# A four-layer network on one core: the first layer's weight fold is moved ahead of the norm and onto ScalarE, and GpSimd builds the convolution matrices

## The chip, the cores and the metric

The kernel runs on one core of a Trainium2 chip. The metric is the device time of one execution in microseconds (us). The five engines of a core have an instruction queue each: TensorE (in profiles PE for matmuls, PEld for its weight loads), VectorE (DVE), ScalarE (ACT), GpSimd (POOL) and SyncE (SP), which here only issues transfers. Each engine takes its own instructions strictly in the order in which they stand in its queue; an instruction that waits for another engine holds up all that stand behind it on its own. Matmul results are in PSUM, which GpSimd doesn't reach in this kernel; VectorE or ScalarE copy them to SBUF.

## What is computed

Sixteen images of 256 channels by 32 x 32 positions go through four layers, all in float32:

```
# layer 0: group norm (8 groups), then self-attention over the 1024 positions
xn = group_norm(x, gamma, beta)
q, k, v = split(einsum('bchw,oc->bohw', xn, w_qkv) + b_qkv)
x = x + w_proj @ (softmax(q^T k / sqrt(C)) v) + b_proj
# layer 1: a gate from the channels' mean and maximum, through two 3x3 convolutions
weight3 = relu(conv3x3(concat([mean, max]), w1, b1))
x = x * sigmoid(conv3x3(mean + max + weight3, w2, b2))
# layer 2: group norm and self-attention again, with weights of its own
# layer 3: attention with 32-wide q and k, logits clipped to [-10, 10], times gamma[0], plus x
```

## The kernel before

**Weights are folded first.** For layers 0 and 2 the kernel works with products of the weights: with M = Wq^T Wk / sqrt(C) the logits are x^T M x, and with Wv and Wproj multiplied beforehand the projection after the attention is gone. `fold(nm, which, base)` makes these once, at the start. `transposed(j)` turns the j-th 256 x 256 weight block (0 is q, 1 is k, 2 is v) on TensorE, four 128 x 128 transposes (L311), and copies the result from PSUM with two VectorE copies (L316). `multiplied` makes a product with eight matmuls as the profile counts them (L322) and scales it out of PSUM with two VectorE instructions (L329). Between them stand `right_sums` (L288 to L291: four sums of weight blocks, on VectorE for M, on GpSimd for the value product), a small bias product `tbp` (L344, scaled at L351) and another, `brp` (L365, added at L372). `fold` is a generator: it yields between its steps.

**Layer 0's norm.** `head(b)` fetches sample b, starts the load of a second copy of it in another layout (`load_tokens`, `xr`), and runs `group_norm`: `bn_stats` over four quarters of the sample on VectorE (L114), a chain of small VectorE instructions that spreads the group's numbers over the partitions (L117 to L134), the power -1/2 on GpSimd (`rstd`, L138), three more small VectorE instructions (L141 to L144), and then the sample itself: channels 0 to 127 on VectorE (L145) and channels 128 to 255 on ScalarE (L146), one instruction of 128 x 1024 each.

**Order.** The order in which instructions are traced is the order that a scheduler starts from; it may bring instructions forward inside an engine's queue, except where `tc.keep_in_program_order` or a dependency added by hand forbids it. `in_turn` runs several generators a step each in rotation. At the very start it runs `head(0)` and `fold("l0", ...)`, so VectorE's queue has the statistics of sample 0 and the copies of the fold interleaved. After that, two streams of samples (even and odd, `stream(0)` and `stream(1)`) run in rotation, together with `later()`, which holds what isn't needed at once: `head(1)` and `fold("l2", ...)`, then `fold3()` (layer 3's weights and biases: `w3qk` copies on GpSimd L410, `bias3` L417 and L426, `qb`, `bcol3` and `strips` L434 to L437 and L380), then `build_toep`, then `checks()`.

**What follows the fold for sample 0.** `attend` makes four sums of sample blocks (`combine`, L909 to L912, tiles `xs` and `x`), then `seven`: each 2 x 2 block product is made with seven products in place of eight (all through L562, tiles `tb`, `ta`, `tc`, `tf` for x^T M, `vb`, `va`, `vc`, `vf` for the values, `sb`, `sa`, `sc`, `sf` for the logits); ScalarE copies some out of PSUM and VectorE adds the others (L612). Then come exponentials (L691, L693) and the weighted values (`weighted`: `b`, `af`, `c`, with sums of exponentials `cb` and others on VectorE, L707, L708, L753, L758).

**The convolution matrices.** The 3 x 3 convolutions of layer 1 are matmuls with 128 x 32 matrices `toep`. `Const.build_toep` builds three of them from the nine taps each: one VectorE instruction per tap (L95: where the index equals the tap, the weight, else 0), one addition for all but the first tap (L98), and three copies of the last matrix (L101). `gate_of` reads them (L169, L182). `n_ok` counts sums in range (L787, L823, L876, on GpSimd); it is read at the end.

**Queues of transfers.** SP issues nearly all; ScalarE's queue has one half of layer 0's weights and half of sample 0 at the start. The sequence on SP is weights of layer 0, sample 0, small constants, sample 1, weights of layers 2 and 3, index tables, and the second copies of samples 0 to 2.

Of the kernel before, what the change touches and what calls it, by code (L numbers as in the profile page):

```python
# [12 lines left out]
AF = mybir.ActivationFunctionType  # L13
ALU = mybir.AluOpType
# [3 lines left out]
C = 256  # L18
CC = C // P
# [37 lines left out]
class Const:  # L57
# [26 lines left out]
    def build_toep(self, tc, work, tidx):  # L84

        nc = tc.nc
        for k in range(3):
            for tap in range(9):
                w = self.sc[:, S_W1 + 9 * k + tap : S_W1 + 9 * k + tap + 1]
                if tap == 0:  # L90
                    one = self.toep[:, k, :]
                else:
                    one = work.tile([P, STRIP], FP, tag="tap", name=f"tap_{k}_{tap}")
                tc.keep_in_program_order(
                    nc.vector.tensor_scalar(one, tidx, float(tap), w, ALU.is_equal, ALU.mult)  # L95
                )
                if tap:
                    nc.vector.tensor_tensor(self.toep[:, k, :], self.toep[:, k, :], one, ALU.add)  # L98
            yield
        for g in range(1, NG):  # L100
            nc.vector.tensor_copy(self.toep[:, 2 + g], self.toep[:, 2])  # L101
        nc.vector.tensor_scalar(self.neg_b2, self.sc[:, S_B2 : S_B2 + 1], -1.0, None, ALU.mult)
        yield


def group_norm(nc, k, small, xt, out, gamma, beta, nm, keep=None):

# [2 lines left out]
    for c in range(CC):  # L112
# [29 lines left out]
    bb = small.tile([P, CC], FP, tag="bb", name=f"bb_{nm}")  # L142
    nc.vector.tensor_tensor(bb, gm, a, ALU.mult)
    nc.vector.tensor_tensor(bb, k.vec[:, :, beta], bb, ALU.subtract)  # L144
    nc.vector.tensor_scalar(out[:, 0], xt[:, 0], a[:, 0:1], bb[:, 0:1], ALU.mult, ALU.add)  # L145
    nc.scalar.activation(  # L146
        out[:, 1], xt[:, 1], AF.Identity, bias=bb[:, 1:2], scale=a[:, 1:2]
    )
    yield


# [50 lines left out]
def fast_path(nc, tc, k, bad, x, w_l0, w_l2, w_l3, qk_bias, v_bias, tap_idx, out):  # L202
# [7 lines left out]
    with ExitStack() as ctx:  # L210
# [83 lines left out]
        def whole(w, nm):  # L294
# [3 lines left out]
            nc.vector.tensor_tensor(full[:, 0, P:], w[:, 1, P:], w[:, 0, P:], ALU.subtract)  # L298
            return full

        def fold(nm, which, base):


# [3 lines left out]
            def transposed(j):  # L307
                for o in range(CC):
                    ps = bank(f"wtp_{nm}_{j}_{o}")
                    for c in range(CC):  # L310
                        nc.tensor.transpose(  # L311
                            ps[:, c * P : (c + 1) * P],
                            w[:, c, j * C + o * P : j * C + (o + 1) * P],
                            k.ident,
                        )
                    nc.vector.tensor_copy(wt[:, j, o, :], ps[:, :C])  # L316

            def multiplied(dst, left, right, scale):
                for c in range(CC):
                    ps = bank(f"fold_{nm}_{c}")  # L320
                    for o in range(CC):
                        nc.tensor.matmul(  # L322
                            ps[:, :C],
                            left[:, o, c * P : (c + 1) * P],
                            right[:, o, :],
                            start=(o == 0),
                            stop=(o == CC - 1),
                        )
                    nc.vector.tensor_scalar(dst[:, c, :], ps[:, :C], scale, None, ALU.mult)  # L329

            transposed(0)
            yield
# [9 lines left out]
            for c in range(CC):  # L342
                for o in range(CC):
# [4 lines left out]
                        start=(o == 0),  # L348
                        stop=(o == CC - 1),
                    )  # L350
            nc.vector.tensor_scalar(tb, ps[:, :CC], C**-0.5, None, ALU.mult)  # L351
            yield
            transposed(2)
            yield
# [582 lines left out]
        def attend(xt, y, weights, lane, nm, then):  # L937
# [39 lines left out]
                then(h, tt.rearrange("p h c n -> p h (c n)"))  # L977
            count(ri, nm)

        def head(b):  # L980

            fetch(b)
# [2 lines left out]
            xr = tokens[b] = load_tokens(b)  # L985
            keep = tc.keep_in_program_order if b == 1 else None
            yield from group_norm(
                nc, k, small, by_chunk, by_chunk, L0_GAMMA, L0_GAMMA + 1, f"l0_{b}", keep
            )
            ready[b] = xt, xr  # L990

# [468 lines left out]
            if first in running:  # L1460
                running.remove(first)

        for _ in in_turn([head(0), fold("l0", 0, L0_GAMMA)]):
            pass


# [328 lines left out]
```

## Time and profile before

| | us |
|---|---|
| median of three runs | 2697.19 |
| lowest and highest of them | 2692.31, 2699.09 |
| the profiled execution | 2694.99 |
| its span in the profile | 2693.2 |
| mean granted TensorE clock in it | 0.997 of full speed |

The span is what the profile covers; the time of an execution has a little around it. The profile's parts that matter here are the busy time of each engine as a share of the span; a table of stages, in which each row is a stretch of time with the busy time and number of instructions of each engine, the granted clock of TensorE and the transfers; the chain of work that ended last, followed back from the end; and the timeline, in which each row has start, duration, engine, line, operation, output<-input, shape and count, and in brackets how long the engine had been idle before and what ended that. Buffer numbers are left out of names, so layer 0's and layer 2's weights are both `raw_l`, and two samples' tiles have one name.

Two more rows of groups help to read what follows (busy time and mean ns of one, after the bar):

```profile
L138 POOL TENSOR_TENSOR rstd_l<-ve_l,neg_half 128x2 f32<-128x2 f32 x32 | 22.2, 695 | 1388.4 <-DVE ve_l L134 1388.4
...
L410 POOL COPY w3qk<-w 128x64 f32<-128x64 f32 x4 | 0.8, 237 | 0.0
```

They are GpSimd's: its work is small, 45.3 us of the span, and its instructions have durations that depend little on their size.

### The profile page before, as it was taken

The page shows a single profiled execution, that of the slowest core. Times are in us where ns is not written, and L with a number is a line of the kernel's source. Part 1 is how long each engine was busy: PE and PEld are TensorE (multiplying, and loading weights), DVE is VectorE, ACT ScalarE, POOL GpSimd, SP SyncE. Part 2 cuts the span into 40 slices and gives each one's busy share as a digit, 9 for nine tenths or more (in the row PEclk, how much of TensorE's full clock was granted, in tenths as well). Part 3 has the DMA queues.
Part 4 walks back from the last instruction along what each step waited for, and adds up shares of the span by engine and source line. Part 5 has one row for each costly group of instructions (what it writes and reads, how often), then busy time and mean ns, then how long its engine had stood idle before and what let it go on. Part 6 is the DMA issues. An engine that isn't in the chain of part 4 may idle for free.

```text
span 2693.2 us, 47725 instructions
## 1 busy us (share of the span) xinstructions
PE 2654.9 (99%) x18998; PEld 2364.0 (88%) x18998; DVE 2152.2 (80%) x4244; ACT 1328.5 (49%) x2813; POOL 45.3 (2%) x118
## 2 busy tenths in 40 slices
PE   7999999999999999999999999999999999999998
PEld 6888988888988889889899898998989889898897
DVE  7988886888778887788867888678886788878777
ACT  3454455544455445544455545455454544545443
POOL 1000000000000000000000000000000000000000
PEclk9999999999999999999999999999999999999999
DMA  4021111212011120211201212112111121101111
GB/s 115 1 63 48 56 32 27 61 48 64 24 47 48 42 77 9 55 48 48 63 15 50 63 33 64 31 33 64 48 48 32 32 64 48 48 17 32 48 40 41
DMA packets 135878, 123.07 MB, mean 46 GB/s; under 512 B 12768, under 2 KB 126688, under 8 KB 135648
## 3 DMA queue, kind: packets, MB, share of 16 engines
q1 hardware_dynamic: 133776, 118.76, 15.9%
q8 instruction: 152, 2.49, 0.4%
q10 hardware_dynamic: 1872, 1.18, 0.1%
q14 instruction: 78, 0.64, 0.1%
HBM read 69.58 MB, written 50.33 MB: 45 GB/s over the span
## 4 chain that ended last, share of the span: by engine, by line
PE 80%; DVE 14%; ACT 3%; issue 2%; DMA 0%; POOL 0%; DVEq 0%; SPq 0%; ACTq 0%
PE b_l L562 15%; PE af_l L562 11%; PE c_l L562 11%; PE sb_l L562 10%; PE sc_l L562 8%; PE sf_l L562 4%; PE sa_l L562 3%; PE vb_l L562 3%; PE tb_l L562 2%; PE s L1099 2%; PE vc_l L562 2%; PE tc_l L562 2%; DVE e_l L612 1%; DVE vt L612 1%; PE qk L1073 1%
## 5 line engine op out<-in xcount | busy, mean ns | idle before, releaser
L681 ACT COPY e_l<-sb_l 128x512 f32<-128x512 f32 x384 | 222.3, 584 | 218.1 <-PE sb_l L562 216.9
L562 PE MATMUL sb_l<-t_l,x 128*128 128x256 f32 x1024 | 262.0, 386 | 0.3
L562 PE MATMUL b_l<-vt,e_l 128*128 128x128 f32 x2048 | 251.8, 275 | 0.0
L562 PEld LDWEIGHTS b_l<-vt,e_l 128*128 128x128 f32 x2048 | 244.2, 192 | 5.4 <-issue 2.3
L562 PEld LDWEIGHTS sb_l<-t_l,x 128*128 128x128 f32 x1024 | 180.5, 191 | 40.1 <-ACT e_l L681 11.2
L691 ACT ACTIVATE e_l<-e_l 128x512 f32<-128x512 f32 x256 | 160.7, 629 | 86.4 <-DVE e_l L612 85.5
L693 ACT ACTIVATE e_l<-e_l 128x1024 f32<-128x1024 f32 x128 | 135.4, 1058 | 118.3 <-DVE e_l L612 118.3
L562 PE MATMUL c_l<-tv,cb_l 128*128 128x129 f32 x1504 | 185.1, 275 | 0.2 <-DVE cb_l L707 0.2
L562 PEld LDWEIGHTS c_l<-tv,cb_l 128*128 128x128 f32 x1504 | 176.6, 191 | 6.9 <-PE qk L1073 3.1
L612 DVE TENSOR_TENSOR e_l<-sc_l,e_l 128x512 f32<-128x512 f32 x128 | 87.7, 685 | 115.3 <-PE sc_l L562 113.6
L478 ACT ACTIVATE xr<-xr,bstrip 128x128 f32<-128x128 f32 (+1 forms) x376 | 134.0, 440 | 43.5 <-DVE xr L485 43.5
L932 ACT COPY vt<-vb_l 128x512 f32<-128x512 f32 x141 | 82.7, 587 | 142.8 <-PE vb_l L562 141.7
L1115 ACT ACTIVATE e<-s 128x512 f32<-128x512 f32 x256 | 132.0, 605 | 28.6 <-PE s L1099 27.9
L562 PE MATMUL af_l<-tv,e_l 128*128 128x128 f32 x1024 | 131.6, 278 | 4.3 <-ACT e_l L691 4.3
L562 PE MATMUL sc_l<-tc_l,xs_l 128*128 128x256 f32 x512 | 133.1, 382 | 2.3 <-DVE vt L612 2.3
L763 ACT COPY acc_l<-c_l 128x256 f32<-128x256 f32 x94 | 34.6, 368 | 201.5 <-DVE ri_l L762 151.7
L562 PE MATMUL sc_l<-t_l,xs_l 128*128 128x256 f32 x512 | 133.0, 382 | 0.8
L562 PE MATMUL sa_l<-t_l,x 128*128 128x256 f32 x512 | 132.1, 380 | 0.0
L1124 DVE TENSOR_SCALAR e<-e 128x1024 f32<-128x1024 f32 x128 | 82.9, 683 | 61.1 <-ACT e L1115 61.1
L562 PE MATMUL sb_l<-tc_l,xs_l 128*128 128x256 f32 x512 | 131.6, 379 | 0.0
L562 PE MATMUL sf_l<-tc_l,x 128*128 128x256 f32 x512 | 131.4, 379 | 0.0
L562 PEld LDWEIGHTS af_l<-tv,e_l 128*128 128x128 f32 x1024 | 121.3, 192 | 10.9 <-ACT e_l L691 7.7
(300 smaller groups left out, 5982.6 us busy)
## 6 DMA issues: line engine op xcount, KB each, us to landing
x<-mid_x SPq DMA_DIRECT2D x64, 512.0 KB, 3.3
xr<-in_x_dram SPq DMA_DIRECT2D x64, 256.0 KB, 5.1
mid_x<-t_z SPq DMA_DIRECT2D x128, 128.0 KB, 2.3
mid_x<-t_l SPq DMA_DIRECT2D x128, 128.0 KB, 2.3
x<-in_x_dram SPq DMA_DIRECT2D x62, 256.0 KB, 3.9
out_dram<-xr SPq DMA_DIRECT2D x124, 128.0 KB, 2.3
raw_l<-in_w_l_dram SPq DMA_DIRECT2D x1, 1024.0 KB, 7.3
raw_l<-in_w_l_dram SPq DMA_DIRECT2D x2, 256.0 KB, 5.5
```

What stands on the lines that cost most here:

```text
L478: nc.scalar.activation(y[:, s, ts], y[:, s, ts], AF.Identity, bias=bias[:, s : s + 1])
L562: mm = nc.tensor.matmul(out, left, right, start=fresh and m == 0 and (lone or i == 0), stop=(m == len(pairs) - 1), skip_group_check=True,)
L612: nc.vector.tensor_tensor(dst, src, dst, ALU.add)
L681: nc.scalar.copy(block(i, j), ps.rearrange("p (m n) -> p m n", m=2))
L691: nc.scalar.activation(part, part, AF.Exp)
L693: nc.scalar.activation(e[:, m : m + 2, :], e[:, m : m + 2, :], AF.Exp)
L763: nc.scalar.copy(acc[:, hi, c2], c[:, :, :P])
L932: nc.scalar.copy(block(i, j), ps.rearrange("p (m n) -> p m n", m=TPH))
L1073: nc.tensor.matmul(ps[i * PH : (i + 1) * PH, : qt * P].rearrange("p (g n) -> p g n", g=qt), w3qk[:, c, i], xt[:, g0 : g0 + qt, c], start=( ...
L1099: nc.tensor.matmul(ss[g][:, j * 2 * P : (j + 1) * 2 * P].rearrange("p (t g j) -> p t g j", t=TPH, g=2), qk[gs, mh, 1 - blk, j * P : (j + 1 ...
L1115: nc.scalar.activation(by_strip[:, :, :, qa], ss[g].rearrange("p (m t n) -> p m t n", m=2, t=TPH), AF.Exp,)
L1124: nc.vector.tensor_scalar(part, part, EXP_MIN, EXP_MAX, ALU.max, ALU.min)
```

## The change

Four things are changed, all at the start of the program:

1. Layer 0's fold is traced as a whole after the first step of `head(0)` (the statistics) and before the rest of it, in place of the rotation.
2. Layer 0's copies and scalings out of PSUM (L316, L329, L351 of the kernel before) are ScalarE instructions. Layer 2's stay on VectorE.
3. Sample 0's normalisation is made in two halves of 128 x 512 on each engine in place of one of 128 x 1024 (`parts` is 2 for sample 0 and 1 for all others), and ScalarE's halves are kept behind the last of the fold's copies of transposed weights (`behind_folds`).
4. `build_toep` is on GpSimd: 27 instructions for the taps, 24 sums and 3 copies.

The ending of the kernel is not touched.

```diff
                 tc.keep_in_program_order(
-                    nc.vector.tensor_scalar(one, tidx, float(tap), w, ALU.is_equal, ALU.mult)
+                    nc.gpsimd.tensor_scalar(one, tidx, float(tap), w, ALU.is_equal, ALU.mult)
                 )
                 if tap:
-                    nc.vector.tensor_tensor(self.toep[:, k, :], self.toep[:, k, :], one, ALU.add)
+                    nc.gpsimd.tensor_tensor(self.toep[:, k, :], self.toep[:, k, :], one, ALU.add)
             yield
         for g in range(1, NG):
-            nc.vector.tensor_copy(self.toep[:, 2 + g], self.toep[:, 2])
+            nc.gpsimd.tensor_copy(self.toep[:, 2 + g], self.toep[:, 2])
...
-def group_norm(nc, k, small, xt, out, gamma, beta, nm, keep=None):
+def group_norm(nc, k, small, xt, out, gamma, beta, nm, keep=None, parts=1, behind=None):
...
-    nc.vector.tensor_scalar(out[:, 0], xt[:, 0], a[:, 0:1], bb[:, 0:1], ALU.mult, ALU.add)
-    nc.scalar.activation(
-        out[:, 1], xt[:, 1], AF.Identity, bias=bb[:, 1:2], scale=a[:, 1:2]
-    )
+    for i in range(parts):
+        ts = slice(i * NT // parts, (i + 1) * NT // parts)
+        nc.vector.tensor_scalar(
+            out[:, 0, ts], xt[:, 0, ts], a[:, 0:1], bb[:, 0:1], ALU.mult, ALU.add
+        )
+        other = nc.scalar.activation(
+            out[:, 1, ts], xt[:, 1, ts], AF.Identity, bias=bb[:, 1:2], scale=a[:, 1:2]
+        )
+        if behind is not None:
+            behind(other)
     yield
...
-                    nc.vector.tensor_copy(wt[:, j, o, :], ps[:, :C])
+                    copy = nc.scalar.copy if nm == "l0" else nc.vector.tensor_copy
+                    copied.append(copy(wt[:, j, o, :], ps[:, :C]))
...
-                    nc.vector.tensor_scalar(dst[:, c, :], ps[:, :C], scale, None, ALU.mult)
+                    if nm == "l0":
+                        nc.scalar.activation(dst[:, c, :], ps[:, :C], AF.Copy, scale=scale)
+                    else:
+                        nc.vector.tensor_scalar(dst[:, c, :], ps[:, :C], scale, None, ALU.mult)
...
-            nc.vector.tensor_scalar(tb, ps[:, :CC], C**-0.5, None, ALU.mult)
+            if nm == "l0":
+                nc.scalar.activation(tb, ps[:, :CC], AF.Copy, scale=C**-0.5)
+            else:
+                nc.vector.tensor_scalar(tb, ps[:, :CC], C**-0.5, None, ALU.mult)
...
+        def behind_folds(ins):
+
+            tc.add_manual_dep(
+                ins.ins,
+                copied[-1].ins.name,
+                mybir.DependencyInfo(
+                    mybir.DependencyClass.NoSync, mybir.DependencyReason.DATA
+                ),
+                reason="the weights' copies come first",
+            )
...
             yield from group_norm(
-                nc, k, small, by_chunk, by_chunk, L0_GAMMA, L0_GAMMA + 1, f"l0_{b}", keep
+                nc,
+                k,
+                small,
+                by_chunk,
+                by_chunk,
+                L0_GAMMA,
+                L0_GAMMA + 1,
+                f"l0_{b}",
+                keep,
+                1 if b else NH,
+                None if b else behind_folds,
             )
...
-        for _ in in_turn([head(0), fold("l0", 0, L0_GAMMA)]):
+        first_head = head(0)
+        next(first_head)
+        for _ in fold("l0", 0, L0_GAMMA):
+            pass
+        for _ in first_head:
             pass
```

More of the change, by code (lines that the diff above doesn't have):

```diff
@@ L299, in whole @@
             return full
+        copied = []
         def fold(nm, which, base):
```

## The prediction

> **What bounds the kernel now.** I read the page's busy shares first, then a table of stages, then the chain and the timeline of the first 70 us.
>
> ```profile
> PE 2654.9 (99%) x18998; PEld 2364.0 (88%) x18998; DVE 2152.2 (80%) x4244; ACT 1328.5 (49%) x2813; POOL 45.3 (2%) x118
> ```
>
> TensorE is busy 2654.9 of 2693.2 us, so only its 38.3 idle us can be won without removing matmuls, and this change removes none. The stages (time, then PE, PEld, DVE, ACT and POOL busy, granted clock, DMA share and GB/s) say where those are:
>
> ```profile
> 0.00:13.40 13.40, 1.95 (x9) 1.58 (x9) 4.95 (x20) 1.28 (x1) 1.57 (x17) 1.00 0.82 238
> 13.40:21.90 8.50, 7.81 (x37) 6.64 (x37) 6.06 (x18) 1.24 (x1) 1.55 (x2) 1.00 0.69 209
> 21.90:48.40 26.50, 26.17 (x152) 20.26 (x151) 24.97 (x66) 11.19 (x20) 4.84 (x9) 1.00 0.53 104
> 48.40:52.00 3.60, 2.11 (x22) 2.01 (x21) 1.25 (x6) 1.94 (x3) 1.23 (x6) 0.92 0.00 0
> 52.00:66.20 14.20, 14.00 (x81) 12.54 (x81) 13.33 (x59) 10.80 (x23) 1.16 (x3) 0.90 0.01 2
> 66.20:115.00 48.80, 48.80 (x309) 42.70 (x310) 47.83 (x118) 19.31 (x40) 1.86 (x5) 1.00 0.00 1
> ```
>
> 11.5 us of idling lie before 13.4 us, 1.5 in the bubble at 48.4 to 52, and next to none from there to 115 us. From 21.9 to 66 TensorE and VectorE are both nearly full; after 66 TensorE has no gap. Who holds up the start is seen in the chain of the first 24 us (start, length, what) and in the timeline:
>
> ```profile
> 9.64 1.29 DVE st_l L114 x2
> ...
> 12.13 0.31 DVE wt_l L316
> ...
> 13.41 3.76 PE fold_l L322 x8
> ```
>
> ```profile
> 4.64 1.94 PE L311 MATMUL wtp_l<-ident,raw_l 128*128 128x128 f32 x8 [4.64 <-DMA raw_l<-in_w_l_dram]
> ...
> 12.05 0.39 DVE L316 COPY wt_l<-wtp_l 128x256 f32<-128x256 f32 x1
> ...
> 14.82 0.81 DVE L145 TENSOR_SCALAR x<-x,a_l,bb_l 128x1024 f32<-128x1024 f32 x1
> ...
> 16.96 1.09 PE L344 MATMUL tbp_l<-vec,wt_l 128*128 128x1 f32 x8
> ...
> 21.89 1.10 PE L562 MATMUL tb_l<-x,m_l 128*128 128x512 f32 x2
> ...
> 23.96 0.69 DVE L612 TENSOR_TENSOR t_l<-ta_l,t_l 128x512 f32<-128x512 f32 x1 [0.18 <-PE ta_l L562]
> ```
>
> The weights are transposed in PSUM at 6.6 us, but their copies stand on VectorE behind statistics that wait for x until 9.64. TensorE idles from 6.6 to 13.4, runs the whole fold after that, and starts sample 0 at 21.89, seven us after its input was normalised.
>
> **The change, part by part.**
>
> *The fold leaves VectorE's queue.* On ScalarE the same copies stand behind its DMA issues (last at 2.56, 0.63 long) and the 1.28 us table load, which no longer waits for x: ready at 4.5. A ScalarE copy of 128x256 from PSUM takes 0.37 (L750, median of 94), VectorE's 0.39. So the last wt copy ends at 7.0 and the fold's matmuls start at 6.7, not 13.4. Then: 3.5 at the pace of the first fold before (cold, 3.78 for eight, against 1.99 for the second one) to 10.2; the bias products need vec, issued at 4.70, landing 5.6 later (10.3), and take 0.9 (11.2); four transposes, whose weights landed 6.9 after their issue at 2.83, 0.6 (11.8); two copies to 12.4; second fold 1.99 (14.3); L365 0.8 (15.1). Sample 0's first matmul can go at 15.1, **6.8 us earlier**. Its input: the norm's small steps lose the four interleaved copies (0.66 of the wait before L145), so L145 goes at 14.16; in halves its first half is there at 14.6, ScalarE's halves (1.24 for the whole) at 14.8 and 15.45. The input is in time. The extra instruction per engine costs about 0.05.
>
> *VectorE keeps up by 5.4 to 6.1.* From 14.16: norm 0.81, four weight sums at 0.2, and sample sums and bias 2.7 at the spacing of before, give L612 at 18.6 instead of 23.96: 5.4 earlier. TensorE now leads, so the waits for it on VectorE at 29.6 and 31.4 (0.3 each) go: 5.9 at sample 1's norm. The weights of layer 2 land at 18.2 (issue 10.89 plus 7.3), before their transposes at 19.2, and sample 1 lands by 16: neither holds it. From there to the second scaling of layer 2's fold the list is the same but for sq (0.6, now later), one tcomb sum (0.35, now earlier) and a wait of 0.4 for that fold. The chain to the bubble (VectorE, GpSimd's sums and copies, bias3, strips) so arrives **5.8 earlier**. The bubble itself stays: it is the chain's own length.
>
> *The matrices leave VectorE.* 27 scalings at 0.145 (spacing; 0.23 each alone), 24 sums at 0.10, 3 copies at 0.11: 6.6 us of VectorE, 5.0 of it before cb, the sum that c_l waits for at 66.16. The order of instructions puts 1.95 of sample 1's sums and sq's 0.6 in that place. But from 52 to 66 TensorE has only 0.4 us of gaps, so this is worth at most **0.4**; its use is slack of about 2.5 us at cb. On GpSimd, 54 operations between copies of 128x64 (0.236) and sums of 128x8 (0.20): 11 to 13 us from about 47.5, longer where they are held up. Behind them stand only the counts n_ok, which nobody awaits; the matrices are first read at 129.5. If that cover were gone, c1_l1 would wait, by what GpSimd runs past about 123.
>
> How such operations meet VectorE's is seen twice:
>
> ```profile
> 22.33 0.90 POOL L291 TENSOR_TENSOR wvp_l<-wvp_l 128x128 f32<-128x128 f32 x1
> ...
> 22.85 0.94 DVE L912 TENSOR_TENSOR x<-x 128x512 f32<-128x512 f32 x1
> ...
> 66.34 1.22 DVE L708 TENSOR_TENSOR e_l<-e_l 128x1024 f32<-128x1024 f32 x1
> 66.50 1.14 POOL L823 TENSOR_TENSOR n_ok<-n_ok,ok_l 128x1 f32<-128x1 f32 x1 [13.34 <-DVE ok_l L822]
> ```
>
> L912 is 0.68 elsewhere and 0.94 here; L823's count is 0.19 to 0.24 elsewhere and 1.14 here, ending with VectorE's L708. So each waits for the other's instruction. A VectorE operation with two SBUF inputs loses at most one matrix operation, 0.2 to 0.24; some 12 to 16 stand in those microseconds, so 2.4 to 3.8 of delay against 6.6 removed: it costs VectorE's slack and no TensorE time. The Trainium skill (SBUF — State Buffer, section Who interferes with whom) says this pair of ports is held exclusively for a whole instruction, which speaks against moving work to GpSimd beside a full VectorE; these rows agree with it.
>
> *No cost elsewhere.* The order of DMA issues is unchanged, and from about the 200th matmul on, every engine's order is that of before, so what is won by 66 us is kept: nothing later is tied to a fixed time.
>
> *Sum:* 5.8 + 0.4 = **6.2 us**. Unknown: after the bubble the first two products ran at 2.07 and 1.54 instead of 1.03 (granted clock 0.90 in that stage), 1.55 us lost; whether this recurs depends on how the bubble falls, so 0 to 1.55 more, or as much less if slow time doubles; I take none. Bounds: 4.5 to 7.8.
>
> **Base.** The profiled execution took 2694.99 (span 2693.2 plus 1.8); the median of three is 2697.19, their spread 6.8. The sum gives 2688.8 from the one, 2691.0 from the other; I say 2690.
>
> **Rivals.**
>
> *More than that.* VectorE follows TensorE by the full 6.8, because more of its small waits before the bubble were for TensorE than I count, and the slow clock after the bubble is spared (1.55): with the 0.4, 8.75 won, 2687 by the middle of the two bases. For it: TensorE has only 0.33 us of gaps in the 26.5 us before the bubble, so it too may set the pace there. Against: the chain runs through VectorE from 29.57 on, and the bubble keeps its length.
>
> *Half is lost at the head.* The second fold runs cold too (3.78 for 1.99), with 0.5 more for waits between ScalarE and TensorE: first matmul at 17.4, and bcol0, in the midst of VectorE's sample sums, holds these up by 1.1; with 2 us of GpSimd delay beyond the slack, 3 are left: 2693. Against: by then TensorE has been busy on and off since 6.7.
>
> *Slower: GpSimd holds VectorE.* GpSimd's slowest elementwise row is rstd, 0.69 for only 128x2. If the matrix operations take that and each meets a VectorE operation, VectorE loses 54 x 0.69 = 37 us up to 100 us, where it is nearly full: less 6.6 removed, 2.5 of slack and the 6.2 won, 22 slower, 2718. It decides from 54 d = 15.3, d = 0.28 per operation; slower by 8 us takes 0.43. Against: 0.20 to 0.24 in the rows of nearest kind (rstd is a power), and not every one will meet.
>
> *It does not do what it says.* If TensorE still waited for x before the fold, nothing is won but 0.4: 2696. Against: in the order of instructions the fold stands first on ScalarE, waiting for TensorE alone.
>
> **How the numbers follow.** The sum as worked 58%; more 20%; a small gain or none 14% (half lost 11, not done 3); slower 8%. 0.3% of this kernel, 8.1 us, is about what a measurement can tell from no change; the line is 2689.1, close to my forecast, and the runs spread over nearly 7 us. So under the line falls some 43% of the first case and 88% of the second: 0.43 faster. Slower by over 0.3%: three quarters of the last, 0.06. The rest, 0.51, within. The range 2684 to 2697 holds the first three cases with a run's spread, and leaves out the slower one and what a lucky clock could add.
>
> **What would show it.** Right: the first fold at about 6.7, tb_l at about 15.1, L612's first at 18.6, bias3 near 43, c_l near 60; GpSimd busy some 12 us more, toep operations at 0.2 to 0.25. Wrong: toep operations above 0.28 with VectorE's xs and cb sums stretched; tb_l after 17; a bubble longer than 3.6; a gain at 66 us that is gone at 500.

## The result and the profile after

| | before | after |
|---|---|---|
| median of 12 runs, us | 2695.47 | 2689.19 |
| lowest and highest | 2692.31, 2699.09 | 2687.49, 2690.09 |
| the profiled execution | 2694.99 | 2688.37 |
| its span | 2693.2 | 2686.6 |
| first and last matmul of `gate_of` in it (TensorE reads `toep`) | 129.5, 2484.9 | 124.1, 2480.2 |

The ratio is 0.9975 with a 95% interval from 0.9966 to 0.9984: 6.3 us less by the medians, 4.3 to 9.2 by the interval. The forecast was 2690, 6.2 less. The lines of the changed kernel are up to 15 further down than those before: L562 is L577, L612 is L627, L912 is L927, L417 is L432 and L380 is L395, but L316 is L325, L344 is L356, L291 is L297, L145 is L147, and L95, L98 and L114 are where they were.

The busy times on the page of the changed kernel:

```profile
PE 2653.6 (99%) x18998; PEld 2362.2 (88%) x18998; DVE 2144.1 (80%) x4180; ACT 1332.6 (50%) x2825; POOL 68.1 (3%) x172
```

TensorE idled 33.0 us, 5.3 less than before; GpSimd's busy time rose by 22.8. The stages, cut where they were cut for before (columns as there):

```profile
0.00:13.40 13.40, 8.27 (x34) 6.60 (x35) 4.28 (x16) 4.36 (x10) 2.26 (x18) 1.00 0.84 240
13.40:21.90 8.50, 8.13 (x36) 4.30 (x36) 8.19 (x21) 4.02 (x7) 2.97 (x4) 1.00 0.74 225
21.90:48.40 26.50, 23.35 (x151) 20.50 (x150) 23.75 (x68) 10.77 (x20) 5.46 (x15) 0.97 0.49 99
48.40:52.00 3.60, 3.60 (x13) 2.99 (x12) 2.29 (x5) 2.68 (x5) 3.19 (x8) 0.72 0.01 5
52.00:66.20 14.20, 14.20 (x110) 13.31 (x109) 13.17 (x23) 10.02 (x24) 12.71 (x23) 1.00 0.01 1
66.20:115.00 48.80, 48.80 (x305) 42.68 (x304) 40.65 (x98) 20.75 (x43) 8.80 (x30) 1.00 0.00 1
```

TensorE is busy 8.27 us of the first 13.4 instead of 1.95: the fold now runs while x is on its way. From 21.9 to 48.4 it idles 3.15 us instead of 0.33, 2.0 of it at bias3 and strips, which have moved into that row, and the rest mostly in layer 2's fold (0.79), for VectorE's copies: TensorE leads now and waits for VectorE. Most of GpSimd's 12.71 and 8.80 us in the last two rows are the matrices (1.16 and 1.86 before).

The start in the timeline of the changed kernel:

```profile
5.26 1.65 ACT L325 COPY wt_l<-wtp_l 128x256 f32<-128x256 f32 x4 [0.76 <-PE wtp_l L319]
...
6.54 3.42 PE L331 MATMUL fold_l<-wt_l 128*128 128x256 f32 x8
...
9.40 1.28 DVE L114 BATCH_NORM_STATS2 st_l<-x 128x6 f32<-128x512 f32 x2 [1.57 <-DMA x<-in_x_dram]
...
12.03 1.99 PE L331 MATMUL fold_l<-raw_l,wt_l 128*128 128x256 f32 x8 [0.24 <-ACT wt_l L325]
...
14.01 1.00 DVE L147 TENSOR_SCALAR x<-x,a_l,bb_l 128x512 f32<-128x512 f32 x2
...
14.67 1.10 PE L577 MATMUL tb_l<-x,m_l 128*128 128x512 f32 x2
...
15.94 0.94 DVE L924 TENSOR_TENSOR xs_l<-x 128x512 f32<-128x512 f32 x1
16.41 0.78 POOL L295 TENSOR_TENSOR vc_l<-wvp_l,vc_l 128x128 f32<-128x128 f32 x1
...
18.02 0.90 POOL L296 TENSOR_TENSOR vc_l<-wvp_l,vc_l 128x128 f32<-128x128 f32 x1
...
19.39 0.68 DVE L627 TENSOR_TENSOR t_l<-ta_l,t_l 128x512 f32<-128x512 f32 x1
```

The first fold starts at 6.54 for 13.41, the first product of sample 0 at 14.67 for 21.89 (7.2 earlier), VectorE's first L627 at 19.39 for 23.96 (4.57 earlier). Between 15.94 and 19.39 VectorE makes the four sample sums at 0.83 to 0.94 each, and GpSimd its four sums for the value product at up to 0.90 each, side by side: 0.68 and 0.46 are what they take alone. bias3 came at 43.88 for 49.05 (5.17 earlier), the first gate matmul 5.4 earlier. The pair of profiles shows 6.6 us between the spans. From the first to the last gate matmul the changed kernel took 0.7 longer, and behind the last one it took 1.9 less (208.3 us to the end before, 206.4 after), in code that was not changed. Nearly all of the 1.9 is TensorE's clock in one place, first of before and then of the changed kernel:

```profile
2649.00:2655.70 6.70, 6.70 (x34) 5.83 (x33) 2.68 (x4) 2.94 (x6) 0.00 (x0) 0.50 0.01 2
```

```profile
2644.60:2647.90 3.30, 3.30 (x16) 2.97 (x15) 0.69 (x1) 1.90 (x4) 0.00 (x0) 0.50 0.03 7
```

Both stretches follow a wait of 2.17 us for VectorE, and in both TensorE was granted half its clock, for 6.7 us in the one and 3.3 in the other; the 3.4 us more at half clock lose 1.7. One pair of profiles doesn't tell what the change is worth by its spans alone.

### The profile page after: what moved, and what is told of

Same layout as the page of the kernel before. It is cut to its first block, busy times and chain, and to the rows that moved or that the text cites. A ratio compares the mean times of both kernels' runs of the same rounds, so it can differ in the third digit from the quotient of the medians.

```text
span 2686.6 us, 47733 instructions
## 1 busy us (share of the span) xinstructions
PE 2653.6 (99%) x18998; PEld 2362.2 (88%) x18998; DVE 2144.1 (80%) x4180; ACT 1332.6 (50%) x2825; POOL 68.1 (3%) x172
## 4 chain that ended last, share of the span: by engine, by line
PE 79%; DVE 14%; ACT 3%; issue 2%; DMA 1%; POOL 0%; DVEq 0%; SPq 0%; ACTq 0%; POOLq 0%
PE b_l L577 15%; PE af_l L577 11%; PE c_l L577 11%; PE sb_l L577 10%; PE sc_l L577 8%; PE sf_l L577 4%; PE sa_l L577 4%; PE vb_l L577 3%; PE tb_l L577 2%; PE s L1135 2%; PE vc_l L577 2%; PE tc_l L577 2%; DVE e_l L627 1%; DVE vt L627 1%; PE qk L1109 1%
## 5 line engine op out<-in xcount | busy, mean ns | idle before, releaser
L577 PE MATMUL sb_l<-t_l,x 128*128 128x256 f32 x1024 | 261.9, 386 | 0.5 <-ACT e_l L696 0.2
L577 PE MATMUL b_l<-vt,e_l 128*128 128x128 f32 x2048 | 251.8, 275 | 0.0
L577 PEld LDWEIGHTS b_l<-vt,e_l 128*128 128x128 f32 x2048 | 244.2, 192 | 5.4 <-issue 2.3
L577 PEld LDWEIGHTS sb_l<-t_l,x 128*128 128x128 f32 x1024 | 180.0, 190 | 40.6 <-ACT e_l L696 11.9
L577 PE MATMUL c_l<-tv,cb_l 128*128 128x129 f32 x1504 | 185.0, 275 | 0.0
L627 DVE TENSOR_TENSOR e_l<-sc_l,e_l 128x512 f32<-128x512 f32 x128 | 87.8, 686 | 118.9 <-PE sc_l L577 117.3
L577 PEld LDWEIGHTS c_l<-tv,cb_l 128*128 128x128 f32 x1504 | 176.6, 191 | 6.5 <-PE qk L1109 3.1
L577 PE MATMUL af_l<-tv,e_l 128*128 128x128 f32 x1024 | 131.5, 278 | 4.3 <-ACT e_l L706 4.3
L577 PE MATMUL sc_l<-tc_l,xs_l 128*128 128x256 f32 x512 | 133.5, 383 | 2.3 <-DVE vt L627 2.3
L577 PE MATMUL sc_l<-t_l,xs_l 128*128 128x256 f32 x512 | 133.0, 382 | 0.8
L577 PE MATMUL sa_l<-t_l,x 128*128 128x256 f32 x512 | 132.3, 381 | 0.0
L577 PE MATMUL sb_l<-tc_l,xs_l 128*128 128x256 f32 x512 | 131.5, 379 | 0.0
L577 PE MATMUL sf_l<-tc_l,x 128*128 128x256 f32 x512 | 131.4, 379 | 0.0
L577 PEld LDWEIGHTS af_l<-tv,e_l 128*128 128x128 f32 x1024 | 121.2, 192 | 10.8 <-ACT e_l L706 7.7
```

Of the source, the lines that this page charges most:

```text
L577: mm = nc.tensor.matmul(out, left, right, start=fresh and m == 0 and (lone or i == 0), stop=(m == len(pairs) - 1), skip_group_check=True,)
L627: nc.vector.tensor_tensor(dst, src, dst, ALU.add)
```

## The experiments

Ten further kernels were run, and the changed one once more. In the table, "x" is the start of VectorE's statistics of the second half of sample 0, which wait for the transfer; "clock" is the granted clock from 40 to 55 us (45 to 60 in before and run 2; the bubble of run 3 lies later still). Times are medians, each ratio is against runs of before on the same chip (medians of 2695.0 to 2695.4 beside the numbered runs), and it is not the quotient of the two medians.

| kernel | us | ratio, 95% | x | tb_l | first L627 | x to L627 | clock | first gate matmul |
|---|---|---|---|---|---|---|---|---|
| before | 2695.47 | | 9.64 | 21.89 | 23.96 | 14.32 | 0.89 | 129.5 |
| changed | 2689.19 | 0.9975 (0.9966 to 0.9984) | 9.40 | 14.67 | 19.39 | 9.99 | 0.89 | 124.1 |
| 1 matrices on VectorE | 2688.67 | 0.9976 (0.9967 to 0.9985) | 9.99 | 16.68 | 19.99 | 10.00 | 0.77 | 125.8 |
| 2 only the matrices | 2694.91 | 1.0003 (0.9994 to 1.0012) | 8.72 | 21.06 | 23.14 | 14.42 | 0.89 | 128.5 |
| 3 copies on VectorE | 2696.80 | 1.0003 (0.9994 to 1.0012) | 8.52 | 23.88 | 27.56 | 19.04 | | 134.4 |
| 4 one part | 2690.85, one run | | 9.88 | 16.95 | 19.69 | 9.81 | 0.89 | 124.2 |
| 5 layer 3's fold later | 2689.39 | 0.9981 (0.9972 to 0.9990) | 10.09 | 15.31 | 20.08 | 9.99 | 1.00 | 124.0 |
| 6 M's sums on GpSimd | 2688.11 | 0.9972 (0.9961 to 0.9983) | 8.72 | 14.42 | 18.47 | 9.75 | 0.77 | 124.2 |
| 7 both of these | 2688.69 | 0.9976 (0.9967 to 0.9985) | 9.63 | 17.78 | 21.61 | 11.98 | 0.90 | 128.2 |
| 8 matrices twice | 2690.22 | 0.9982 (0.9972 to 0.9991) | 8.67 | 14.92 | 18.71 | 10.04 | 0.77 | 125.3 |
| 9 bubble filled | 2688.84 | 0.9977 (0.9968 to 0.9986) | 9.30 | 14.55 | 19.29 | 9.99 | 1.00 | 122.7 |
| 10 the changed kernel again | 2687.51, one run | | 8.77 | 14.20 | 18.76 | 9.99 | 0.89 | 123.4 |
| 11 filled, M's sums on GpSimd | 2688.84 | 0.9980 (0.9971 to 0.9989) | 9.39 | 15.09 | 19.14 | 9.75 | 1.00 | 122.5 |

Three of the programs lie at 2694.9 to 2696.8 (before, 2, 3), all others at 2687.5 to 2690.9. What divides them is whether layer 0's fold leaves PSUM through ScalarE. All that have ScalarE's copies have the new tracing order too, so whether that order is needed beside them is not shown.

**1. The matrices back on VectorE.** The changed kernel with the three calls of `build_toep` on `nc.vector`:

```diff
-                    nc.gpsimd.tensor_scalar(one, tidx, float(tap), w, ALU.is_equal, ALU.mult)
+                    nc.vector.tensor_scalar(one, tidx, float(tap), w, ALU.is_equal, ALU.mult)
...
-                    nc.gpsimd.tensor_tensor(self.toep[:, k, :], self.toep[:, k, :], one, ALU.add)
+                    nc.vector.tensor_tensor(self.toep[:, k, :], self.toep[:, k, :], one, ALU.add)
...
-            nc.gpsimd.tensor_copy(self.toep[:, 2 + g], self.toep[:, 2])
+            nc.vector.tensor_copy(self.toep[:, 2 + g], self.toep[:, 2])
```

> The changed kernel with build_toep back on VectorE; the fold as changed. Theory (the head start of the fold is the gain, the matrices give at most 0.4 us): the gate's first matmul at 124.1 to 124.6 in the profile (129.5 before, 124.1 changed), time within 1 us of the changed kernel, 6 us below the one before. Rival (the 6.6 us taken from VectorE are a good half of the gain): the gate's first matmul at 126.5 to 128, time 3 us above the changed kernel.

It took 2688.67, as the changed kernel does. The whole gain is there without GpSimd. The gate came at 125.8, outside what was expected: x landed 0.59 later than in the changed kernel, and the clock behind the bubble was 0.77. From L627 to the gate it took 105.8 us; run 6, with the matrices on GpSimd and the same clock, took 105.7.

**2. The matrices on GpSimd alone.** The kernel before with the opposite edit in `build_toep` and nothing else.

> The kernel before with build_toep on GpSimd and nothing else. Theory: the gate's first matmul at 129.0 to 129.5, time within 1 us of the kernel before. Rival (VectorE's relief is a good half of the gain): first matmul at 126 to 127.5, time 3 us below. Second rival (GpSimd's 0.40 us operations hold VectorE up): first matmul after 130, time above.

It took 2694.91, ratio 1.0003: no gain. Its profile began 0.9 us earlier only because x landed earlier (8.72 for 9.64); from there to L612 it took 14.42, as before. The wait of 0.20 us for cb at c_l was gone, and c_l came 0.14 earlier after L612. What else the move did is seen in the row of 75.3 to 110 us, of before and of this run (total, then PE, PEld, DVE, ACT, POOL busy, clock, transfers):

```profile
75.30:110.00 34.70, 34.70 (x209) 29.43 (x208) 34.09 (x76) 15.72 (x32) 0.68 (x3) 1.00 0.00 0
```

```profile
75.30:110.00 34.70, 34.70 (x209) 29.43 (x207) 30.24 (x71) 15.39 (x30) 3.96 (x15) 1.00 0.00 1
```

VectorE works 3.9 us less in it, and TensorE was and is busy for the whole of it: here slack was made longer, and nothing else.

**3. The new order with VectorE's copies.** The changed kernel, but layer 0's copies and scalings are VectorE's, and the dependency by hand is left out:

```diff
-                    copy = nc.scalar.copy if nm == "l0" else nc.vector.tensor_copy
+                    copy = nc.vector.tensor_copy
...
-                    if nm == "l0":
+                    if False:
...
-            if nm == "l0":
+            if False:
...
-                None if b else behind_folds,
+                None,
```

> The changed kernel with layer 0's copies and scalings on VectorE again (and without the dependency behind them); the fold is still traced ahead, the matrices are on GpSimd. Theory (the engine that copies is what counts, since the scheduler puts the copies behind the statistics in VectorE's queue whatever the tracing): first fold matmul at 12.8 to 13.5, tb_l at 21 to 22, the gate's first matmul at 128.5 to 129.5, time as before. Rival (tracing the fold ahead gives the gain): tb_l before 17, first gate matmul at 124 to 125.

2696.80, ratio 1.0003, so nothing is left of the gain, though the profiled execution was slower at the start than expected (first gate matmul at 134.4). Its timeline:

```profile
10.93 0.39 DVE L325 COPY wt_l<-wtp_l 128x256 f32<-128x256 f32 x1
...
12.27 3.78 PE L331 MATMUL fold_l<-wt_l 128*128 128x256 f32 x8 [5.58 <-DVE wt_l L325]
...
18.74 3.78 PE L331 MATMUL fold_l<-raw_l,wt_l 128*128 128x256 f32 x8 [0.23 <-DVE wt_l L325]
...
23.88 2.05 PE L577 MATMUL tb_l<-x,m_l 128*128 128x512 f32 x2
...
27.56 0.69 DVE L627 TENSOR_TENSOR t_l<-ta_l,t_l 128x512 f32<-128x512 f32 x1 [2.00 <-PE ta_l L577]
```

The copies stand behind the statistics again, although the fold is traced first: the first of them starts 2.41 us after x, as before (12.05 less 9.64). In this execution the second fold and the first products ran at half pace too (3.78 for 1.99, 2.05 for 1.10), and VectorE waited 2.00 for TensorE.

**4. The norm in one part.** In the changed kernel, sample 0's `parts` is 1:

```diff
-                1 if b else NH,
+                1,
```

> The changed kernel with sample 0 normalised in one instruction per engine. Theory: VectorE saves the 0.2 us that the second instruction costs but TensorE's first product waits for the whole, 0.4 us; tb_l at 14.9 to 15.1, xs sums at 15.8, the gate's first matmul within 0.3 of 124.1. Rival (the halves are part of the gain): tb_l after 15.5 and the gate's first matmul at 124.6 or later.

The first product came at 16.95, not at 15, for another reason than the one tested: the second fold ran at the cold pace.

```profile
12.62 3.49 PE L331 MATMUL fold_l<-raw_l,wt_l 128*128 128x256 f32 x8 [0.24 <-ACT wt_l L325]
...
16.95 1.10 PE L577 MATMUL tb_l<-x,m_l 128*128 128x512 f32 x2
...
19.69 0.68 DVE L627 TENSOR_TENSOR t_l<-ta_l,t_l 128x512 f32<-128x512 f32 x1
```

This miss told most. TensorE was 2.3 us later than in the changed kernel, and L627 came 9.81 after x, where the changed kernel takes 9.99: nothing was lost, and the 0.18 are what one instruction in place of two saves VectorE. Runs 1 and 10 show the same interval, 10.00 and 9.99, with TensorE at 16.68 and 14.20. From x's landing to L627 it is VectorE's own list that counts; TensorE has over 2 us to spare.

**5. Layer 3's fold later.** The changed kernel with one line more ahead of `fold3()`:

```diff
+            yield from wait(3)
             fold3()
```

> The changed kernel with one line more: layer 3's fold starts three steps later, so that bias3's products stand on TensorE behind three products of the next group of logits. In the changed kernel TensorE idles 1.17 us ahead of bias3 and 0.84 ahead of strips, and the five products behind them take 1.9 us more than at the usual 1.03 each (granted clock 0.72). Theory (the head's time is a chain through this bubble, and the slow clock is its consequence): the products of the moved group cover what bias3 waits for, both the idling and the slow clock go, up to 3.9 won and 1 kept for strips: first gate matmul near 121 for 124.1, time near 2686.0 for 2689.2. Rival (VectorE sets the pace in this stage, the bubble only shows its lag): TensorE waits as long a few products later, first gate matmul within 0.7 of 124.1, time 2688.5 to 2689.5.

2689.39, and the gate at 124.0. bias3 moved behind three of the next products and still waited 1.45 for GpSimd's copies; the wait ahead of strips and the slow clock went (1.00 from 40 to 55), but TensorE then waited 0.83 and 0.32 at 73 to 75 us for VectorE's operands of the bounds (`reach`, `reachb`). From L627 to the gate it took 103.9 us for 104.7: 0.8 of the 3.1 hoped for, and in the time nothing that shows. Neither theory had it whole.

**6. M's sums on GpSimd.** 

```diff
-            mc = right_sums(nc.vector, m, f"mc_{nm}")
+            mc = right_sums(nc.gpsimd if nm == "l0" else nc.vector, m, f"mc_{nm}")
```

> The changed kernel with the four sums of layer 0's M taken from VectorE to GpSimd, which has none of the fold's work until 15.9 us. Theory (VectorE, not TensorE, sets the pace from 14 to 42 us): the four sums, 0.85 us between the norm and the sample sums, go, so the first combining instruction on VectorE comes at 18.5 for 19.39, bias3 at 43.0 for 43.88, the first gate matmul at 123.3 for 124.1; time about 2688.3. Rival (TensorE sets the pace): the first product stays at 14.7, bias3 within 0.3 of 43.88, no gain; or GpSimd's sums last longer than TensorE's way to the first product (four at 0.5 to 0.9), and tb_l comes later.

L627 came at 18.47, as VectorE's pace would have it, but 0.68 of the 0.92 us are x's landing at 8.72 for 9.40: the interval shrank by 0.24 only. The four sums, 1.01 us of VectorE's list, were gone from it, but on GpSimd they stood at 12.67 to 14.67, beside the norm: VectorE's small instructions ahead of it took 0.39 longer (L141 0.41 for 0.16, L144 0.30 for 0.16), its two halves 1.24 for 1.00, and then VectorE waited 0.31 for ScalarE's half. The clock behind the bubble was lower (0.77), and the gate no earlier. The time, 2688.11, can't be told from 2689.19.

**7. Both together.**

> The two edits together: layer 3's fold three steps later, and M's sums on GpSimd. If both theories hold the gains add, as one shortens the chain ahead of the bubble and the other takes the bubble away: first gate matmul near 120.2, time near 2685.2. If VectorE's pace is all there is, it gives what the sums on GpSimd give alone, about 2688.3; if TensorE's, what the moved fold gives alone, about 2686.0.

2688.69. Its profile, of the longest of its eleven executions (2692.80), caught the start that the prediction's second rival described:

```profile
10.39 1.26 PE L356 MATMUL tbp_l<-vec,wt_l 128*128 128x1 f32 x8 [1.34 <-DMA vec<-in_vecs_dram]
...
12.65 3.78 PE L331 MATMUL fold_l<-raw_l,wt_l 128*128 128x256 f32 x8
...
17.78 2.06 PE L577 MATMUL tb_l<-x,m_l 128*128 128x512 f32 x2
...
21.61 0.69 DVE L627 TENSOR_TENSOR t_l<-ta_l,t_l 128x512 f32<-128x512 f32 x1 [1.44 <-PE ta_l L577]
```

TensorE idled 1.34 for vec, ran the second fold and sample 0's first products at half pace, and VectorE waited 1.44 for it: L627 came 11.98 after x, 2 us late. So a cold second fold by itself is free (runs 1 and 4), and costs from the point where the products after it are cold as well.

**8. The matrices built twice.** In the changed kernel `later()` runs `build_toep` a second time, with the same values:

```diff
             yield from k.build_toep(tc, work, tidx)
+            yield from k.build_toep(tc, work, tidx)
```

> The changed kernel with the convolution matrices built twice on GpSimd, one after the other, with the same values: 54 instructions more, from about 75 to 102 us at the pace of the first (0.40 per tap, 0.25 per sum, and waits), when VectorE is busy and GpSimd has little else. Theory (GpSimd does the waiting, VectorE's instructions are lengthened by 0.01 to 0.08 each): VectorE's busy time from 75 to 110 rises by less than 1 us, the first gate matmul stays within 0.5 of 124.1, time within 1 of 2689.2. Rival (each instruction of GpSimd holds VectorE for its own length): 54 instructions at 0.25 to 0.40 are 17 us of VectorE, more than its slack of about 5 us in that stretch, so the first gate matmul comes 8 to 12 later and the time is 2697 to 2701.

The stretch from 75 to 115 us, of this kernel and of the changed one:

```profile
75.00:115.00 40.00, 40.00 (x255) 34.82 (x254) 32.47 (x80) 15.81 (x26) 22.69 (x56) 1.00 0.00 1
```

```profile
75.00:115.00 40.00, 40.00 (x254) 34.80 (x253) 31.88 (x80) 16.88 (x31) 1.39 (x8) 1.00 0.00 1
```

GpSimd worked 21.3 us more, VectorE 0.6, TensorE had no gap in either. The gate came at 125.3, outside the 0.5 expected, and from L627 on it took 106.6 us for 104.7, 1.9 more. All of that lies ahead of 60 us, and the second building begins only behind 73: after the bubble TensorE had half its clock for 6.8 us and not for 3.4 (the rows are under run 9), which puts the products behind it back by 1.4, and TensorE waited 0.55 for ScalarE's e_l at 58.16, where TensorE's order differs from the changed kernel's (`size_l` stands behind c_l). The time, 2690.22, is 1.0 above the changed kernel's, within what the intervals leave open. The rival asked for 2697 at least.

**9. The bubble filled.** The changed kernel with products that nobody reads in TensorE's waits at bias3 and strips:

```diff
             ps = bank("bias3")
+            for _ in range(7):
+                nc.tensor.matmul(
+                    ps[:, P : P + 2 * DQK], k.ident, w3[:, 0, : 2 * DQK], start=True, stop=True
+                )
...
             ps = bank(f"strips_{nm}")
+            for _ in range(3 if nm == "l3" else 0):
+                tc.keep_in_program_order(
+                    nc.tensor.matmul(ps[:, P : 2 * P], k.ident, k.ident, start=True, stop=True)
+                )
```

> The changed kernel with ten products more on TensorE whose results nobody reads: seven of 128x64 stand ahead of bias3 and three of 128x128 ahead of strips, in what is idling in the changed kernel (1.17 and 0.84 us). Nothing else is moved, except that half a product of the next logits goes ahead of strips. From VectorE's first L627 to the first gate matmul the changed kernel took 104.7 us, and that with M's sums on GpSimd 105.7; from 40 to 55 us the granted clock was 0.89 and 0.77. Theory (the idling itself brings the slow clock): clock 1.00 from 40 to 55, all five products behind the bubble at 1.03 to 1.11, and the stretch takes 102.5 to 103.5; time 1.5 to 2 below the changed kernel. Rival (the clock goes slow at moments that this kernel does not set): the clock from 40 to 55 is as low as 0.77 to 0.92 again, the stretch 104.5 to 106, time as the changed kernel or 0.5 above it.

The bubble of the changed kernel, in the timeline:

```profile
43.88 0.60 PE L432 MATMUL bias<-bcol,w3qk 128*128 128x1 f32 x4 [1.17 <-POOL w3qk L425]
...
46.22 0.41 PE L395 MATMUL strips_l<-bcol,ident 128*32 128x2 f32 x8 [0.84 <-DVE bcol L452]
...
46.56 1.68 PE L577 MATMUL sb_l<-t_l,x 128*128 128x256 f32 x4
...
48.04 1.91 PE L577 MATMUL sa_l<-t_l,x 128*128 128x256 f32 x4
...
49.75 1.36 PE L577 MATMUL sc_l<-tc_l,xs_l 128*128 128x256 f32 x4
```

Behind it the granted clock was 0.50, and 1.00 on both sides, for 3.4 us in the changed kernel and for twice that in run 8:

```profile
47.00:50.40 3.40, 3.40 (x10) 2.68 (x9) 2.05 (x6) 1.94 (x3) 3.23 (x9) 0.50 0.03 7
```

```profile
45.20:52.00 6.80, 6.44 (x22) 5.22 (x23) 4.86 (x13) 2.34 (x4) 5.97 (x14) 0.50 0.02 5
```

And filled (the profile counts each of the seven and of the three as two):

```profile
42.72 1.77 PE L436 MATMUL bias<-w,ident 128*128 128x64 f32 x14
44.33 0.56 PE L440 MATMUL bias<-bcol,w3qk 128*128 128x1 f32 x4
...
46.92 0.41 PE L399 MATMUL strips_l<-bcol,ident 128*32 128x2 f32 x8
47.26 0.70 PE L585 MATMUL sb_l<-t_l,x 128*128 128x256 f32 x2
47.80 1.03 PE L585 MATMUL sa_l<-t_l,x 128*128 128x256 f32 x4
48.66 1.03 PE L585 MATMUL sc_l<-tc_l,xs_l 128*128 128x256 f32 x4
```

The fill delays bias3 by 0.45 and strips by 0.70, and yet sc_l starts 1.09 earlier, because the products behind the bubble run at 1.03 instead of 1.36 to 1.91. The granted clock from 40 to 55 is 1.00 here and in run 11, and 0.77 or 0.89 in all six profiles of the new start in which the bubble was left as it is: 6.8 or 3.4 us at half the clock. From L627 to the gate it took 103.4 in both, for 104.5 to 106.6 in those six. That the idling brings the slow clock is shown; the Trainium skill says the same (TensorE: Matmul & The Clock Gate, What's actually happening: the clock is set by how busy the array has lately been). Its table puts the half clock behind an idle window of about 3.4 us; here two waits of 2.0 us together, with one-column products between them, were enough. But the time did not follow, 2688.84. The 1.3 us are less than the interval can tell, and the eleven executions differ by more: five with a mean granted clock of 0.999 took 2687.4 to 2688.2 us, three with 0.997 took 2690.9 to 2693.4, while the changed kernel's twelve, all at 0.997 or 0.998, took 2687.5 to 2690.1. Where the longer ones lost their clock no profile shows. Run 11 shows another loss.

**10. The changed kernel once more.**

> The changed kernel once more, for the spread of one program between executions. If the small differences between the runs so far are the clock's and the transfers' and not the edits', the second fold may take 1.99 or 3.4 to 3.8, the first sample product come anywhere from 14.4 to 17, the clock from 40 to 55 be 0.77 to 0.90, and the span differ from 2686.6 by up to 2.5 us with every instruction in the same order. If these are fixed by the program, it repeats 14.7, 1.99, 0.89 and 2686.6 within 0.5 us.

x landed at 8.77 for 9.40 and all that follows came 0.5 to 0.7 earlier, the gate at 123.4, the span was 2685.7; the second fold and the clock (1.99, 0.89) were those of the first profile. So the two executions of one program differ by x's landing; the other paces are seen between programs with the same start.

**11. Filled, and M's sums on GpSimd.**

> The changed kernel with the filled bubble and with M's four sums on GpSimd. If the idling brings the slow clock and VectorE sets the pace ahead of the bubble, both gains add: first L627 near 18.5, the first gate matmul near 121.5, time 2686.0 to 2687.5 for 2689.2. If the clock goes slow by itself, 2688 as with the sums on GpSimd alone.

L627 came at 19.14 for 18.5, as M's sums won only the 0.24 of run 6. The gate was the earliest of all, 122.5, for 121.5, and the time 2688.84 for 2686.0 to 2687.5 expected. In the two profiles the head's gain was spent in the body: from the first to the last gate matmul it took 2358.0 us, and 2356.9 in run 9, for 2355.3 to 2356.5 in the others. The samples' gates come in pairs, and from one pair to the next it takes 282.6 us in most places; here it was 283.3, 282.9 and 284.4 in three. The last of these places in the timeline of this kernel:

```profile
1939.57 2.57 SPq L249 DMA_DIRECT2D x<-in_x_dram  x4
...
1944.58 0.69 DVE L114 BATCH_NORM_STATS2 st_l<-x 128x6 f32<-128x512 f32 x1 [1.81 <-DMA x<-in_x_dram]
...
1953.67 2.45 ACT L501 ACTIVATE xr<-xr,bstrip 128x128 f32<-128x128 f32 x8 [4.83 <-DVE xr L508]
...
1959.68 2.05 PE L585 MATMUL c_l<-vt,e_l 128*128 128x129 f32 x16 [0.94 <-ACT acc_l L786]
```

The next sample's x is issued at 1939.57 and its statistics, the next thing in VectorE's queue, started 5.0 us later; where nothing is lost they start 3.1 after the issue. VectorE is held 1.81, ScalarE behind it, and TensorE 0.94. There are seven places of this kind. This run had such waits at three of them (0.69, 0.37, 1.81), run 9 at the same three (0.49, 0.28, 0.65), the changed kernel at two (0.34, 0.16), each other run at one at most, and of 0.45 at most. The two earliest heads have by far the longest waits; that the earlier head makes them likelier can't be told from two executions, but that they take back what it wins, in these two, is in the lines. Nothing was run to issue x earlier.

No version can be told from the changed kernel: the medians of all that keep its fold lie between 2688.1 and 2690.2, in intervals that overlap with its own.

## Why the prediction was right, step by step

**The time: right, and nearer than the sum deserves.** 6.2 us were forecast, 6.3 measured, 4.3 to 9.2 by the interval. In the profiles c_l came at 60.77 for 66.16, 5.4 earlier for the 6.2 of the sum, and so did the first gate matmul. From x on that is 5.2: to the gate it took 119.9 us before and 119.8 in run 2, 114.7 in the changed kernel and 114.6 in run 10. What makes 6.3 of it in the medians isn't located and can be chance, so the match to 0.1 is luck in part.

**TensorE 6.8 earlier: right and not what counts.** 7.2. The first fold took the 3.5 that were reckoned (3.42), the second 1.99. The prediction didn't put this lead into its sum but followed VectorE's own list from the norm, and that was right: runs 1, 4 and 10 show the lead to be spare by more than 2 us. Before, VectorE waited for the fold on the way to L612 (0.91, 0.46, 0.29 and 0.29 us); after, x's transfer and VectorE's list set its time.

**VectorE 5.4 to L612: mis-sized, 4.57, or 4.33 from x on** (14.32 less 9.99). The norm started at 14.01 for 14.16, with x 0.24 earlier, so from x on 0.09 late. From there to L627 it took 5.38 for the 4.44 reckoned: norm in halves 0.92 for 0.81, M's sums 1.01 for 0.8, sample sums and bias 3.45 for 2.7 (these terms of the prediction add up to 4.31; its 18.6 has 0.13 more). The last is the term that was mis-sized: the sample sums meet GpSimd's value sums, which the fold's move brings forward to 15.9 to 18.9. Before, two of the four met them (L911 0.78, L912 0.94, the first two 0.68 each); after, all four did. The prediction had the very pair in its fence (L912 at 0.94 beside L291 at 0.90) and used it for the matrices, not for the sums that the fold takes along. In run 7 the sums at 16.19 and 18.04 cost VectorE 0.69 and 0.68 where GpSimd's instruction came second, and 0.94 where GpSimd's was already under way.

**0.4 more up to the bubble: about right,** 0.60 (L627 to bias3 24.49 us, 25.09 before). Together bias3 came 5.17 earlier for 5.8.

**The bubble and its clock: the idling stays; the slow clock is a consequence, of varying size.** TensorE idles 2.0 us in it for 1.5 before. The prediction took 1.55 us lost as unchanged and gave -1.55 to 1.55 as its bounds. Half the clock for 3.4 us loses 1.7 (before, the changed kernel, runs 2, 4 and 10), for 6.8 us 3.4 (runs 1, 6 and 8), and nothing is lost where the bubble was filled: the bounds, a loss of 0 to 3.1, were of about the right size, and that the loss was the same before and after is luck.

**The matrices: no value, right; the cost on GpSimd, wrong by half.** At most 0.4 was given to VectorE's relief; run 2 has 0.14 of it at c_l, and the times of runs 1 and 2 show nothing. The operations were put at 0.20 to 0.25 and 11 to 13 us in all; undisturbed, a tap took 0.40, a sum 0.25 and a copy 0.21, 17 us in all, and the whole stood from 47.9 to 75.2, 27 us:

```profile
L95 POOL TENSOR_SCALAR tap<-tidx,sc x24: 394/398/1655, 48.3 to 73.9; 128x32 f32<-128x32 f32 x24
```

The columns are the least, median and longest in ns. The nearest rows were of other operations, and GpSimd's sums do grow with their size: 0.25 for 128x32, 0.45 for 128x128. The other 10 us are waiting, and GpSimd does it:

```profile
51.34 0.69 DVE L924 TENSOR_TENSOR xs_l<-x 128x512 f32<-128x512 f32 x1
51.68 0.46 POOL L98 TENSOR_TENSOR toep<-toep,tap 128x32 f32<-128x32 f32 x1
52.06 0.69 DVE L925 TENSOR_TENSOR xs_l<-xs_l,x 128x512 f32<-128x512 f32 x1
52.22 1.31 POOL L95 TENSOR_SCALAR tap<-tidx,sc 128x32 f32<-128x32 f32 x1
52.68 0.68 DVE L927 TENSOR_TENSOR x<-x 128x512 f32<-128x512 f32 x1
```

The sample sums of sample 1, back to back, keep their 0.68 to 0.69, and the tap beside them takes 1.31 and ends with the last of them. So the 2.4 to 3.8 us of delay for VectorE did not come either (sq, 0.76 for 0.68, is the most that one instruction lost). Nothing hung on it: the cover named for GpSimd, 129.5 us until the matrices are read, was wide enough.

**The rivals.** GpSimd holding VectorE was to decide from 0.28 per operation; the taps do exceed that, but VectorE isn't held by them for their length, and run 8 doubles them for 0.6 us of VectorE. Half lost at the head happens: of the ten profiles with ScalarE's copies three had a cold second fold (runs 1, 4 and 7), and only run 7 lost by it. More than 6.2 needed VectorE to follow TensorE; it follows x. That the change doesn't do what it says would have come true without ScalarE: run 3 is that kernel.

## What to carry to other kernels

When the cause of a late start is taken away, look for what comes next in line before adding up the lead: here the arrival of the input and one engine's list after it, against which 2 us of TensorE's earliness were worth nothing. Moving a stage moves what it issues on other engines too, and a pair that interfered once in the old trace can do so wherever the two now lie side by side. And a difference of a few us between two profiles should be split at a landmark behind the change: of 6.6 us here 1.9 lay in untouched code, most of it in how long TensorE's clock stayed at half, and an edit that won 1.3 at the landmark had lost it by the end of its two profiles.

## What the runs showed of the hardware

- The same start has several paces. The changed kernel and run 1 have the same instructions until the matrices begin at 46.7 us, and the second fold took 1.99 in the one and 3.41 in the other. In the three profiles with a slow second fold TensorE had waited 0.88 to 1.34 us for `vec` shortly before it (runs 1, 4, 7), in the other seven with ScalarE's copies 0.46 at most. It goes with that wait and not with the transfer alone: in run 5 `vec` came as late as in run 1 (10.82 and 10.84), but the first fold lasted 3.78 there for 3.07, and the second took 2.00. Over all profiles x landed between 8.52 and 10.09.
- TensorE's slow clock behind a bubble is half the clock, and it lasts longer than the bubble's idling (2.0 us): 3.4 us in the changed kernel and 6.8 in run 8, and the three products after the bubble ran at up to 1.91 for 1.03. Filling the wait with useless products removed it, in both runs that tried it.
- GpSimd and VectorE in each other's way: GpSimd's small operations wait for a full VectorE (0.40 becomes 1.31), while GpSimd's 128x128 sums, with VectorE's sample sums coming one after another, cost each of these up to 0.26 us. The Trainium skill (SBUF — State Buffer, Who interferes with whom) says that whoever issues first holds the shared ports for its whole instruction; the rows agree as far as who came first waited less. Why VectorE's next sum came first each time beside the taps, and not beside the 128x128 sums, no run here tells.
